# Value products by half columns and another dealing of probability copies in an attention kernel

## The chip, the cores and the metric

The kernel runs on one core of a Trainium2 chip. The metric is the device time of one execution in microseconds (us), as the median of several runs. One further execution was taken with the hardware profiler; every duration below is from it.

The core has five engines that run side by side, each in its own order, and wait for each other through semaphores: PE (TensorE, matrix products; its weight loads are listed apart as PEld), DVE (VectorE), ACT (ScalarE), POOL (GpSimd) and SP (SyncE, which issues most of the DMA transfers).

## The reference, cut to what matters

The input `x` holds 32 sequences of 32 tokens with 512 features. Three conditional layers are added to it one after another (a mixing by a picked matrix, a linear layer with a picked low-rank part, a linear layer with a picked weight). The fourth layer is attention with a paged cache, and the change lies in it:

```python
q = jnp.einsum('bsd,ed->bse', x, Wq).reshape(bsz, seqlen, HQ, D)   # HQ = 32 heads of D = 128
k = jnp.einsum('bsd,ed->bse', x, Wk).reshape(bsz, seqlen, HK, D)   # HK = 8
v = jnp.einsum('bsd,ed->bse', x, Wv).reshape(bsz, seqlen, HK, D)
# q, k: rms norm and rotary position
k_all = jnp.concatenate([kc, k], axis=1)      # 512 cached keys, then the 32 new ones
v_all = jnp.concatenate([vc, v], axis=1)
scores = jnp.einsum('bqhd,bkhd->bhqk', q, k_all) * SCALE
scores = jnp.where(valid[:, None, None, :], scores, -1e+30)
probs = jax.nn.softmax(scores, axis=-1)
o = jnp.einsum('bhqk,bkhd->bqhd', probs, v_all)
return jnp.einsum('bse,de->bsd', o, Wo)
```

All arithmetic is in float32. A float32 product appears in the trace as two matmul records.

## The kernel before, in words

**Stages.** The tokens are 1024 rows, held as 8 token tiles of 128 (`x3t`). The first part of the span computes the three conditional layers, then the projections to queries, keys and values. From 373.5 us on the attention runs. The projections are cut into chunks of 512 columns; the last chunk holds half of the values. Of that chunk only token tiles 0 and 1 are projected ahead of attention. Tiles 2 to 7 are projected inside it, as "fills": four products (one for each 128 of the 512 input features) that add up in one PSUM bank, the tile `qkv` with tag `f`. ACT copies the bank to `vs` (line 318), and SP stores `vs` to DRAM two steps later (line 323). That tag has one buffer, so the first product of the next token tile waits for ACT's copy.

**Steps.** Attention goes through 256 units, one for each batch b (32) and key head g (8), in the loop at line 1248; step n = 8b + g. All engines follow the order written in the loop. In step n:

- PE computes the scores of unit n: one product of 288 columns (line 1019) and one of 256 (line 1020) into `s_ps`, which has one buffer, so that the next scores wait until DVE has read it.
- DVE adds the mask and finds the row's least value, `low` (line 1028); ACT takes the exponential into `pr` (line 1044). Four units make a quad, so a batch has two quads, q = 0 and 1.
- On steps n < 37 PE does the fill, if there is one (`fill`, line 1231).
- For the quad that was finished before step n - n % 4, the piece j = n % 4 is turned: DVE transposes 32 x 32 blocks of all four units into `turned` (line 1057), and four copies, one for each group of 32 partitions, put them into `placed` in their right places (`place`, line 1052). The copies are dealt out to ACT (line 1069), POOL (line 1071) and DVE (line 1073). `turned` has two buffers.
- POOL gathers the probabilities of the new keys when j = 0 (`pq`, line 1080), and PE flips them when j = 2 (line 1084).
- From step 37 on PE does a share of the output projection (line 1174), most often one product of 512 columns a step.
- From step 8 on PE does the values of unit n - 8: four products of 128 columns (line 1097), with `placed` as the weights. So the values of step 8b + 8 are the first to need quad 0 of batch b, whose last piece is turned in step 8b + 7; those of step 8b + 12 need quad 1, whose last piece is turned in step 8b + 11.
- After the fourth unit of a quad PE adds the new values (line 1117, in steps 8b + 3), and DVE computes `rden` (line 1131) and scales the result into `os` (line 1133). The PSUM banks of a batch's result are one buffer, so the first values of the next batch wait for `os`. In the next step or later DVE transposes `os` to `ot` (line 1154). In the last step of a batch DVE writes the `mask` of the next (line 218).
- From batch 2 on POOL issues four index DMAs in steps 8b to 8b + 3, one for each chunk of the cached values `vt` (line 252); the first waits until the values of batch b - 2 have been used.

**The fills before.** There are 24 products of 512 columns. Steps 0 to 9 have one each, then the odd steps from 11 to 35 and step 36; the even steps from 10 to 34 are in `EMPTY` and have none.

**The copies before.** Of the four copies of a piece, ACT does the first `on_act`; the rest go to POOL (quad 0, and all of batch 0) or DVE. With one letter a copy (A ACT, P POOL, D DVE): quad 0 is A A P P, quad 1 A A D D and its last piece A A A D; in batch 0 it is A P P P and A A P P.

Of the kernel before, what the change touches and what calls it, by code (L numbers as in the profile page):

```python
# [20 lines left out]
P = 128  # L21
B, S, HID = 32, 32, 512
# [5 lines left out]
NT = B * S // P  # L28
BT = P // S
KC = HID // P  # L30
# [4 lines left out]
NCH = (HQ + 2 * HK) // REP  # L35
# [3 lines left out]
QUAD = 4  # L39
# [20 lines left out]
def cond_resid_kernel(  # L60
# [237 lines left out]
    def x3t(t: int):  # L298
        return x3_all[:, :, t * P : (t + 1) * P]
# [5 lines left out]
    ws = {}  # L305
# [2 lines left out]
        ws[c] = wqps[c % 2].tile([P, KC, HID], F32, tag="wq", name=f"wq_{c}")  # L308
        eng.dma_start(out=ws[c], in_=w_qkv[c])

    def project_part(ps, c: int, t: int, k: int):
        nc.tensor.matmul(
            ps, x3t(t)[:, k, :], ws[c][:, k, :], start=(k == 0), stop=(k == KC - 1)
        )

    def copy_values(ps, c: int, t: int):
        vs = vsp.tile([P, HID], F32, tag="vs", name=f"vs_{c}_{t}")
        nc.scalar.copy(vs, ps)
        return vs
# [5 lines left out]
    def project(c: int, t: int, slots=()):  # L325
        ps = accumulator(f"qkv_{c}_{t}", True)
        for k in range(KC):
            project_part(ps, c, t, k)
        for slot in slots:
            flush(slot)  # L330
        store_values(copy_values(ps, c, t), c, t, nc.gpsimd)
# [720 lines left out]
    def place(b: int, q: int, j: int):  # L1052
        if j == 0:
            placed[b, q] = tp.tile([P, QUAD, L // P, P], F32, tag="placed", name=f"placed_{b}_{q}")
        pr = prs[b, q][:, :, :L].rearrange("p u (c j s) -> p j u c s", j=P // S, s=S)[:, j]
        part = tp.tile([P, QUAD, L // P, S], F32, tag="turned", name=f"turned_{b}_{q}_{j}")
        nc.vector.transpose(part, pr)  # L1057

        on_pool = q == 0 or b == 0
        if b == 0:  # L1060
            on_act = 1 + q
        else:
            on_act = 3 if q == 1 and j == QUAD - 1 else 2
        for i in range(P // S):
            dst = placed[b, q][j * S : (j + 1) * S, :, :, i * S : (i + 1) * S]
            src = part[i * S : (i + 1) * S]
            dst, src = (a.rearrange("p u c s -> p (u c) s") for a in (dst, src))
            if i < on_act:
                nc.scalar.copy(dst, src)  # L1069
            elif on_pool:  # L1070
                nc.gpsimd.tensor_copy(dst, src)  # L1071
            else:
                nc.vector.tensor_copy(dst, src)  # L1073
# [129 lines left out]
    LAG = 8  # L1203
# [17 lines left out]
    units = [(b, g) for b in range(B) for g in range(HK)]  # L1221
    N = len(units)

    fills = [(t, k) for t in range(2, NT) for k in range(KC)]
    FILLED = 37
    EMPTY = tuple(n for n in range(LAG + 2, FILLED) if n % 2 == 0)
    EMPTY = EMPTY[: FILLED - len(fills)]
    filled, unstored = {}, {}
    WO_AT = [*range(7, 35, 3), *range(FILLED + 4, FILLED + 16, 2)]

    def fill(n: int):
        if n < FILLED and n not in EMPTY:
            t, k = fills.pop(0)
            if k == 0:
                filled[t] = ps_p.tile([P, HID], F32, tag="f", name=f"qkv_{NCH - 1}_{t}")
            project_part(filled[t], NCH - 1, t, k)
            if k == KC - 1:
                unstored[n + 2] = copy_values(filled.pop(t), NCH - 1, t), NCH - 1, t, nc.sync

    order = {  # L1240
# [6 lines left out]
    with tc.manual_schedule(engines=order):  # L1247
        for n in range(N + LAG):
            b, g = divmod(n, HK)
# [8 lines left out]
            if n < N:  # L1258
# [21 lines left out]
                exponentials(*scored)  # L1280
            flip_kept(n)
            fill(n)
            if n in unstored:
                store_values(*unstored.pop(n))
# [4 lines left out]
            if QUAD <= n < N + QUAD:  # L1289
                bq, i = divmod(n - QUAD, HK)  # L1290
                q, j = divmod(i, QUAD)
                if j == 0:
                    gather_new(bq, q)
                if j == 2:
                    flip_new(bq, q)
                place(bq, q, j)
# [89 lines left out]
```

## Time and profile before

| | |
|---|---|
| median of 3 runs | 1139.4 us (1138.61 to 1139.44) |
| profiled execution: time, span | 1139.8 us, 1138.0 us |
| granted TensorE clock | 1.0 |
| busy share of the span | PE 99%, PEld 64%, DVE 71%, ACT 66%, POOL 49% |
| attention begins, step 8, step 37 | 373.5 us, 390.66 us, 469.31 us |

The span is the time from the first to the last instruction that the profile shows; the execution's own time has 1.8 us around it. Matmuls overlap, and the end of one is modelled, so the distance from one start to the next tells more of PE than a duration. In a row of a timeline the brackets name how long the engine was idle before it and what ended that. In a group's row stand the count, the busy time, the mean of one in ns, and the idle time of the engine just before the group.

### The profile page before, as it was taken

Reading aid. Unit: us, or ns where it says so; the run is one execution under the profiler, and the core shown is the slowest. Engines: PE = TensorE matmul, PEld = TensorE weight load, DVE = VectorE, ACT = ScalarE, POOL = GpSimd, SP = SyncE. Lnnn points to the kernel's source line nnn. Section 1 sums busy time; section 2 is a strip of 40 time slices with the busy share of each in tenths; the row PEclk is TensorE's granted clock in tenths of the full one; section 3 lists DMA queues with packets and bytes.
Section 4 is the critical chain, followed back from the end, with each engine's and each line's share of the span. In section 5 each row is a group of like instructions: output and inputs, shape, how many; then the busy total and the mean of one; then the engine's idle time right before and its main releaser. Section 6 shows DMA issues by size and latency. Waiting matters only on the chain. (4 is left out here: it accounts for less than half of the span.)

```text
span 1138.0 us, 18994 instructions
## 1 busy us (share of the span) xinstructions
PE 1122.4 (99%) x5432; PEld 730.1 (64%) x5432; DVE 807.5 (71%) x1670; ACT 752.8 (66%) x1900; POOL 559.0 (49%) x719
## 2 busy tenths in 40 slices
PE   8999999999999999999999999999999999999998
PEld 5554444444444577777777777777777777777766
DVE  2510688886977487777778868877877777877851
ACT  1211377576666688777777777877777877777750
POOL 3411689899897544533443344334533443344310
PEclk9999999999999999999999999999999999999999
DMA  8998447688786587888667756765776676766610
GB/s 319 392 419 347 176 133 220 174 234 229 197 232 169 159 272 267 271 308 284 216 217 243 248 190 230 262 229 178 243 251 223 200 239 224 240 202 214 222 29 10
DMA packets 173354, 259.24 MB, mean 228 GB/s; under 512 B 31522, under 2 KB 130466, under 8 KB 168770
## 3 DMA queue, kind: packets, MB, share of 16 engines
q1 hardware_dynamic: 152226, 184.22, 51.0%
q0 software_dynamic: 20016, 71.97, 17.7%
q10 hardware_dynamic: 1008, 1.84, 0.4%
q8 instruction: 44, 0.72, 0.3%
q14 instruction: 60, 0.49, 0.1%
HBM read 228.46 MB, written 37.88 MB: 234 GB/s over the span
## 5 line engine op out<-in xcount | busy, mean ns | idle before, releaser
L1069 ACT COPY placed<-turned 32x512 f32<-32x512 f32 x539 | 332.8, 617 | 31.4 <-DVE turned L1057 24.0
L1097 PEld LDWEIGHTS o_ps<-vt,placed 128*128 128x128 f32 x2048 | 267.0, 191 | 118.5 <-issue 89.4
L1028 DVE CUSTOM_DVE_ANT_0 pr<-s_ps,mask,rq 128x544 f32<-128x544 f32 x256 | 200.6, 784 | 132.5 <-PE s_ps L1020 124.0
L1044 ACT ACTIVATE pr<-pr,low 128x544 f32<-128x544 f32 x256 | 192.2, 751 | 132.7 <-DVE low L1028 130.8
L1071 POOL COPY placed<-turned 32x512 f32<-32x512 f32 x268 | 163.6, 611 | 230.8 <-DVE turned L1057 164.1
L1097 PE MATMUL o_ps<-vt,placed 128*128 128x128 f32 x2048 | 270.4, 275 | 5.6 <-ACT placed L1069 2.8
L1174 PE MATMUL f_ps<-wo,ot 128*128 128x512 f32 x480 | 241.3, 594 | 0.7
L1057 DVE STREAM_TRANSPOSE turned<-pr 128x512 f32<-128x512 f32 x256 | 178.7, 698 | 0.1
L1019 PE MATMUL s_ps<-kt,qt 128*128 128x288 f32 x512 | 174.4, 422 | 1.4 <-DVE low L1028 0.5
L1020 PE MATMUL s_ps<-kt,qt 128*128 128x256 f32 x512 | 152.3, 379 | 0.4 <-issue 0.4
L252 POOL DMA_INDIRECT vt<-in_v_cache_dram,v_idx x128 | 128.0, 1000 | 36.6 <-issue 25.4
L1020 PEld LDWEIGHTS s_ps<-kt,qt 128*128 128x128 f32 x512 | 97.2, 190 | 27.5 <-DMA kt<-in_k_cache_dram 0.8
L434 POOL TENSOR_TENSOR ra<-ra,rs 128x512 f32<-128x512 f32 x80 | 103.9, 1306 | 10.6 <-DVE rs L429 6.4
L1174 PEld LDWEIGHTS f_ps<-wo,ot 128*128 128x128 f32 x480 | 85.8, 190 | 28.6 <-issue 13.9
L1073 DVE COPY placed<-turned 32x512 f32<-32x512 f32 x217 | 94.6, 436 | 5.5
L1080 POOL COPY pq<-pr 128x128 f32<-128x128 f32 x64 | 18.6, 290 | 149.4 <-PE o_ps L1097 94.6
L447 ACT ACTIVATE sq<-x 128x128 f32<-128x128 f32 x256 | 76.4, 302 | 19.3 <-DVE x L405 13.9
L1019 PEld LDWEIGHTS s_ps<-kt,qt 128*128 128x128 f32 x512 | 77.3, 191 | 17.0 <-DVE low L1028 10.6
L544 ACT COPY r<-m 128x512 f32<-128x512 f32 x80 | 46.4, 580 | 52.4 <-PE m L389 51.4
L389 PE MATMUL m<-t_pair,x_sums 128*128 128x512 f32 x160 | 75.3, 593 | 0.6 <-ACT r L544 0.6
L389 PE MATMUL m<-w_pair,x3t 128*128 128x512 f32 x160 | 75.2, 592 | 0.0
L389 PE MATMUL m<-w_pair,x_sums 128*128 128x512 f32 x160 | 72.1, 592 | 0.0
(129 smaller groups left out, 1223.6 us busy)
## 6 DMA issues: line engine op xcount, KB each, us to landing
kt<-in_k_cache_dram SPq DMA_DIRECT2D x512, 128.0 KB
wa<-in_w_adapt_dram SPq DMA_DIRECT2D x32, 1024.0 KB
q_d<-st SPq DMA_DIRECT2D x128, 128.0 KB
qt<-q_d SPq DMA_DIRECT2D x64, 256.0 KB
w_pair<-in_w_qkv_dram SPq DMA_DIRECT2D x20, 512.0 KB
o_d<-in_w_o_dram SPq DMA_DIRECT2D x16, 512.0 KB
wo<-o_d SPq DMA_DIRECT2D x16, 512.0 KB
k_d<-st SPq DMA_DIRECT2D x32, 128.0 KB
```

Source lines behind the costliest of these rows:

```text
L252: nc.gpsimd.indirect_dma_start(out=vts[b][:, c, :], out_offset=None, in_=v_cache, in_offset=bass.IndirectOffsetOnAxis(ap=v_idx[:, at : at ...
L389: nc.tensor.matmul(ps, of[:, k], by[:, k], start=(not more and k == 0), stop=(k == KH - 1), skip_group_check=more,)
L434: nc.gpsimd.tensor_tensor(u.a, u.a, u.s, ALU.add)
L1019: nc.tensor.matmul(ps[:, first:L], q, kt4[:, :N_LOW, g, :], start=True, stop=True)
L1020: nc.tensor.matmul(ps[:, L : first + LT], q, kt4[:, N_LOW:, g, :], start=True, stop=True)
L1028: nc.vector.tensor_tensor_reduce(pr, ps[:, first : first + LT], mask, rqs[b][:, g // QUAD, u : u + 1], 3.0e38, ALU.add, ALU.min, low,)
L1044: nc.scalar.activation(pr, pr, AF.Exp, bias=low, scale=-1.0, accum_out=dens[quad][:, u : u + 1])
L1057: nc.vector.transpose(part, pr)
L1069: nc.scalar.copy(dst, src)
L1071: nc.gpsimd.tensor_copy(dst, src)
L1097: nc.tensor.matmul(po, pt[:, c, :], vt[:, c, g * D : (g + 1) * D], start=(c == 0 and q == 0), stop=(c == L // P - 1 and q == 1),)
L1174: nc.tensor.matmul(pfs[t][:, :HID], ots[t, h // HALF][:, h % HALF, :], wo(h), start=(h == 0), stop=(h == (HQ if t < NT - 1 else HALF) - 1),)
```

## The change

Each product of the fills is done in two halves of 256 columns, first all four of the left half of a token tile, then all four of the right half, in the same PSUM bank. There are now 48. Every step from 0 to 36 has one, and steps 0 to 7, 8, 16 and 24 have two. ACT's copies to `vs` are now in steps 3, 7, 14, 21, 28 and 36; they were in steps 3, 7, 13, 21, 29 and 36. The first half product of the next token tile follows in the very next step.

In batches 0 to 4 the four copies of a piece are dealt out otherwise: quad 0 is A P P P with the last piece A D D P, quad 1 is A A P P. So in each of batches 1 to 4 ACT does 12 copies where it did 17, DVE 2 where it did 7, and POOL 18 where it did 8. In batch 0 only the last piece of quad 0 differs. From batch 5 on all is as before.

The orders of the engines differ in nothing else, but that SP's store of `vs` of one token tile stands one step later, behind the key loads of a batch.

```diff
-    def project_part(ps, c: int, t: int, k: int):
+    def project_part(ps, c: int, t: int, k: int, cols=slice(0, HID)):
         nc.tensor.matmul(
-            ps, x3t(t)[:, k, :], ws[c][:, k, :], start=(k == 0), stop=(k == KC - 1)
+            ps[:, cols],
+            x3t(t)[:, k, :],
+            ws[c][:, k, cols],
+            start=(k == 0),
+            stop=(k == KC - 1),
         )
...
-        on_pool = q == 0 or b == 0
-        if b == 0:
-            on_act = 1 + q
+        if b <= BT:
+            by = "AAPP" if q == 1 else "ADDP" if j == QUAD - 1 else "APPP"
+        elif q == 0:
+            by = "AAPP"
         else:
-            on_act = 3 if q == 1 and j == QUAD - 1 else 2
+            by = "AAAD" if j == QUAD - 1 else "AADD"
         for i in range(P // S):
...
-            if i < on_act:
+            if by[i] == "A":
                 nc.scalar.copy(dst, src)
-            elif on_pool:
+            elif by[i] == "P":
                 nc.gpsimd.tensor_copy(dst, src)
             else:
                 nc.vector.tensor_copy(dst, src)
...
-    fills = [(t, k) for t in range(2, NT) for k in range(KC)]
+    fills = [(t, h, k) for t in range(2, NT) for h in range(2) for k in range(KC)]
     FILLED = 37
-    EMPTY = tuple(n for n in range(LAG + 2, FILLED) if n % 2 == 0)
-    EMPTY = EMPTY[: FILLED - len(fills)]
+    DOUBLE = (*range(LAG), 8, 16, 24)
...
     def fill(n: int):
-        if n < FILLED and n not in EMPTY:
-            t, k = fills.pop(0)
-            if k == 0:
+        for _ in range((1 + (n in DOUBLE)) * (n < FILLED)):
+            t, h, k = fills.pop(0)
+            if (h, k) == (0, 0):
                 filled[t] = ps_p.tile([P, HID], F32, tag="f", name=f"qkv_{NCH - 1}_{t}")
-            project_part(filled[t], NCH - 1, t, k)
-            if k == KC - 1:
+            project_part(filled[t], NCH - 1, t, k, slice(h * HID // 2, (h + 1) * HID // 2))
+            if (h, k) == (1, KC - 1):
                 unstored[n + 2] = copy_values(filled.pop(t), NCH - 1, t), NCH - 1, t, nc.sync
```

## The prediction

> **What bounds the kernel now.** I read the page first, then the windows over the stretch that the change touches, then the timelines of TensorE, VectorE and GpSimd around one batch border, then the answer on the tile `placed`.
>
> The page: engine totals and the groups of the copies that are dealt out anew.
>
> ```profile
> PE 1122.4 (99%) x5432; PEld 730.1 (64%) x5432; DVE 807.5 (71%) x1670; ACT 752.8 (66%) x1900; POOL 559.0 (49%) x719
> ...
> L1069 ACT COPY placed<-turned 32x512 f32<-32x512 f32 x539 | 332.8, 617 | 31.4 <-DVE turned L1057 24.0
> ...
> L1071 POOL COPY placed<-turned 32x512 f32<-32x512 f32 x268 | 163.6, 611 | 230.8 <-DVE turned L1057 164.1
> ...
> L1073 DVE COPY placed<-turned 32x512 f32<-32x512 f32 x217 | 94.6, 436 | 5.5
> ```
>
> PE fills 99% of the span, so only PE's idle time or PE's work can change the time. A copy costs 617 ns on ACT, 611 on POOL, 436 on DVE. The windows (steps 8 to 15, 16 to 23, 24 to 31, 32 to 36; then a stretch that the change does not touch on PE):
>
> ```profile
> 390.66:412.18 21.52, 21.04 (x124) 15.94 (x125) 13.69 (x30) 17.23 (x36) 11.70 (x21) 1.00 0.73 225
> 412.18:434.00 21.82, 19.79 (x124) 15.47 (x123) 17.58 (x38) 18.33 (x37) 9.51 (x15) 1.00 0.79 271
> 434.00:455.27 21.27, 20.11 (x124) 15.54 (x123) 17.70 (x38) 17.91 (x37) 9.50 (x15) 1.00 0.91 306
> 455.27:469.31 14.04, 13.16 (x85) 10.14 (x84) 12.81 (x28) 11.37 (x23) 5.77 (x8) 1.00 0.89 312
> 469.31:490.00 20.69, 20.69 (x121) 15.41 (x120) 15.48 (x35) 16.23 (x35) 9.50 (x14) 1.00 0.81 271
> ```
>
> Length, then busy time of PE, PEld, DVE, ACT, POOL. The last window has no idle PE; the four before it have 4.55 us (78.65 less 74.10). Where it lies, PE's timeline shows (steps 15 and 16):
>
> ```profile
> 410.00 0.59 PE L1020 MATMUL s_ps<-kt,qt 128*128 128x256 f32 x2
> 410.44 1.02 PE L312 MATMUL qkv<-wq,x3t 128*128 128x512 f32 x2
> 411.29 1.05 PE L1097 MATMUL o_ps<-vt,placed 128*128 128x128 f32 x8
> 412.18 0.65 PE L1019 MATMUL s_ps<-kt,qt 128*128 128x288 f32 x2
> 412.67 0.59 PE L1020 MATMUL s_ps<-kt,qt 128*128 128x256 f32 x2
> 414.30 1.13 PE L1097 MATMUL o_ps<-vt,placed 128*128 128x128 f32 x8 [1.04 <-ACT placed L1069]
> ```
>
> Starts, not durations, give PE's price, since matmuls overlap: a whole fill 0.85 us (410.44 to 411.29; 0.86 elsewhere), values 0.89, scores 0.92 (with a 256-column pair at 0.43), a flip 0.11. Step 16 has no fill, and its values wait 1.04 us for the last copies of `placed`. DVE and POOL at that border:
>
> ```profile
> 411.34 0.71 DVE L1057 STREAM_TRANSPOSE turned<-pr 128x512 f32<-128x512 f32 x1
> 411.98 0.14 DVE L1131 RECIPROCAL rden<-den 128x4 f32<-128x4 f32 x1
> 412.38 0.69 DVE L1133 TENSOR_TENSOR os<-o_ps,rden 128x512 f32<-128x512 f32 x1 [0.27 <-PE o_ps L1097]
> 412.99 0.69 DVE L218 TENSOR_SCALAR mask<-key_i,len_f 128x544 f32<-128x544 int16 x1
> 413.81 0.78 DVE L1028 CUSTOM_DVE_ANT_0 pr<-s_ps,mask,rq 128x544 f32<-128x544 f32 x1
> ```
>
> ```profile
> 412.11 1.27 POOL L1071 COPY placed<-turned 32x512 f32<-32x512 f32 x2 [0.80 <-DVE rden L1131]
> 413.65 1.02 POOL L252 DMA_INDIRECT vt<-in_v_cache_dram,v_idx  x1 [0.27 <-POOL placed L1071]
> 414.72 0.29 POOL L1080 COPY pq<-pr 128x128 f32<-128x128 f32 x1
> 415.18 1.06 POOL L252 DMA_INDIRECT vt<-in_v_cache_dram,v_idx  x1 [0.17 <-issue]
> 416.55 0.94 POOL L252 DMA_INDIRECT vt<-in_v_cache_dram,v_idx  x1 [0.30 <-issue]
> ```
>
> Here lie the two things that decide: DVE is nearly solid from the transpose to the next `low`, and POOL has four index DMAs in each batch from the third on, each about 1.0 us busy with 0.3 between.
>
> **Part 1, the halves.** 24 products become 48 of half the columns. By the 256-column scores row a half takes 0.43, so 48 of them cost what 24 whole ones do (0.86): nothing is added. Each loads its weights again; eight value matmuls in 0.89 us already load weights at that pace, so the loads stay covered; without that cover it is at most 24 times two loads of 0.19, 9 us, which I exclude as the narrower 128-column row does not show it. Steps 0 to 8 keep the same work. From 9 to 36 a step costs 0.92 + 0.43 + 0.89 = 2.24, with a flip 2.35, with the new values 2.99 (0.65, and 0.10 that PE loses in starting afresh, as after each wait: 414.30 to 415.27 is 0.97 for 0.89). Before, it was 2.67 with a fill; without, 1.97 to 2.07, since the next scores wait for `low` (its start 1.12 after the scores', its result 0.84 later).
>
> The accumulator has one buffer, so the next chunk's first half waits for ACT's copy `vs`. Chunks now end at 14 and 21 with the next at 15 and 22 (before, a step lay between). ACT does the exponential first: it starts 1.94 after the scores, takes 0.84, the copy 0.57: 3.35. PE is there at 3.27 and 3.16: with latency and restart +0.25 in step 15, +0.35 in 22. Behind that fill PE's values and scores queue. A chunk's end at 28 hides behind the wait of that step (below). Of SP only one store of `vs` moves behind a batch's loads; its rows are read from batch 16 on: nothing.
>
> **Part 2, the copies.** In batches 1 to 4 each batch takes five copies from ACT (3.1 us), five from DVE (2.2) and gives POOL ten (6.1). None is on PE; what counts is when the fourth piece of a quad is ready. Two borders per batch:
>
> *Into step 8b* (letters A D D P). From the scores of 8b-1: `low` starts at 1.12, the transpose at 1.83, ends at 2.54; the two DVE copies, new here, 0.85: 3.39; reciprocal 0.14, `os` 0.69: 4.22; mask 0.50; `low` 4.72; scores of 8b+1 at 5.56. Values of 8b wait for `os` too (same PSUM banks), to 4.3, where before ACT's second copy came last. A DVE copy beside a POOL copy is in no row. Bounds: 0 and 0.61 (one POOL copy first, twice in the worst case). Nearest: the mask, 0.50 in its eight uses beside no POOL copy and 0.70 in the 24 beside one. I take 0.20: 5.76, rounded to 5.8 for the two steps, against 5.85, 5.42 and 5.55 measured at 16, 24 and 32. So this wait is not removed; it passes from ACT to DVE. What is gained is that the doubles at 16 and 24 lie under it.
>
> *Into step 8b+4* (A A P P instead of A A A D). ACT's third copy goes. POOL now alternates: index DMA 0.3 + 1.0, two copies 1.27: 2.57 a step against PE's 2.24 to 2.99. From the scores of 8b (24 or 32): `low` at 2.7, `ot` and the transpose, done at 4.8; copies of the first piece done at 6.1; then three times 2.57: 13.85. PE: 3.56 + 2.34 + 2.35 + 2.99 + 1.35 = 12.59. So the values of 28 and 36 wait 1.3 for POOL, and behind them queue PE's next scores, on which `low` and the exponential wait. At 20 `ot` falls away: 12.9 against 12.3, 0.6. Step 12 has no DMAs: 0.04 as before. Step 44 is covered by whole output products (2.67 a step). The fourth `vt` chunk is issued about 12 us after step 8b starts and lands 6.3 to 8.7 later, before the 22.5 or so at which it is read.
>
> At step 8 the last piece drops two POOL copies: it is ready at 392.7 instead of 393.4, PE comes at 392.97: 3.20 instead of 3.78.
>
> **The sum**, steps before against after:
> - 8 to 15: 21.52; 3.20 + 2.24 + 2.35 + 2.99 + 2.28 + 2.24 + 2.35 + 2.50 = 20.15: -1.37
> - 16 to 23: 21.82; 3.30 + 2.34 + 2.35 + 2.99 + 2.94 + 2.24 + 2.70 + 2.24 = 21.10: -0.72
> - 24 to 31: 21.27; 3.56 + 2.34 + 2.35 + 2.99 + 3.64 + 2.24 + 2.35 + 2.24 = 21.71: +0.44
> - 32 to 36: 14.04; 3.56 + 2.34 + 2.35 + 2.99 + 3.64 = 14.88: +0.84
>
> Together -0.8 us: span 1138.0 to 1137.2, the profiled execution 1139.8 to 1139.0. Its time lies 0.4 above the median 1139.4, so the forecast is 1138.6.
>
> [...] The mask shows 0.46 at its fastest, 0.69 at the median over its 32 uses. [...]
>
> **Rivals.**
> - *POOL keeps up.* If the 0.3 between DMAs hides beside copies and these take 0.61, its turn is 2.22: ready at 12.75, wait 0.16 instead of 1.3, none at 20: -3.1 further, 1135.5. For it: the 0.3 is issue time, not work. Against: it stood there with POOL otherwise idle.
> - *PE alone bounds.* Without any wait steps 8 to 36 need 19.22 three times and 11.96: 69.6 against 78.65, so 1130.4. Against: DVE's 5.56 at three borders alone.
> - *POOL is slower than its median* (the other side). Its place is steps 16 to 19, 24 to 27, 32 to 35. With copies at 0.70 (three took 2.11 at 391.29, beside a mask) and DMAs at 1.19 + 0.3 (longest in these batches), its turn is 2.89, the waits 1.7, 2.35 and 2.35 instead of 0.6, 1.3, 1.3: +3.2, so 1141.8. It decides from about 2.65 on (slower than before); from 2.88 by more than can be measured.
> - *It comes out even*: the gains of part 1 and the borders cancel, 1139.4.
>
> **How the numbers follow.** Three runs lie within 0.83 us; 0.2%, 2.3 us, is about what a measurement of this kernel can tell from no change. Forecast 0.48, even 0.17, POOL keeps up 0.18, PE alone 0.05, POOL slower 0.12. Faster by over 2.3 us: POOL keeps up, PE alone and the lower edge of the forecast, 0.26; slower by over 2.3: most of the slow-POOL case, 0.10; within 0.64. The range runs from POOL keeping up (1135.3) to most of the slow case (1141.3); DVE's bound of 0.61 at three borders (+1.2) lies inside.
>
> **What would show it.** Right: in steps 9 to 36 fills of 128x256 at 0.43 from start to start; steps of 2.24 inside a batch; PE idle at 16, 24 and 32 ended by DVE `os`, at 20, 28 and 36 by POOL's `placed`, about 0.6 and 1.3 long; steps 37 on unchanged. Wrong: no POOL wait at 28 and 36 (then faster), DVE copies of 0.6 and more beside POOL's, half fills costing over 0.5, or `vt` landing late at 24, 32 or 40.

## The result and the profile after

The changed kernel takes 1209.9 us (median of 5 runs, 1209.45 to 1212.13) beside 1139.4 us for the kernel before (5 runs, 1138.61 to 1139.67): ratio 1.0622, 95% interval 1.0611 to 1.0634. The forecast was 1138.6. The change costs 70 us where nearly nothing was expected. The profiled execution of the changed kernel took 1212.1 us, its span is 1210.3, and its mean granted clock 0.972.

The page of the changed kernel: the engine totals, the granted clock over the span in 40 slices of 30 us, and the groups of copies.

```profile
PE 1131.2 (93%) x5480; PEld 745.9 (62%) x5480; DVE 800.9 (66%) x1652; ACT 739.0 (61%) x1880; POOL 581.8 (48%) x757
...
PEclk9999999999999977887999999999999999999999
...
L1074 ACT COPY placed<-turned 32x512 f32<-32x512 f32 x519 | 319.8, 616 | 72.2 <-DVE turned L1061 63.7
L1076 POOL COPY placed<-turned 32x512 f32<-32x512 f32 x306 | 187.0, 611 | 297.1 <-DVE turned L1061 175.0
L1078 DVE COPY placed<-turned 32x512 f32<-32x512 f32 x199 | 88.0, 442 | 5.1
```

PE's busy time has risen by 8.8 us only, the span by 72.3. A POOL copy still costs 611 ns; POOL is busy 22.8 us more, far from 72. So no work has become dear: PE stands idle. Where, the steps tell. Starts of steps after, less before: +0.4 us at step 8, -0.8 at 16, then +19.0 at 24, +37.4 at 32, +55.1 at 40, +72.4 at 48, and it stays there to the end. The loss lies in four batches, and in each of them nearly all in one step: 20, 28, 36 and 44 take 22.27, 19.51, 19.47 and 18.78 us. The four windows of the prediction became 20.31 (forecast 20.15), 41.62 (21.10), 39.70 (21.71) and 31.04 (14.88).

PE's timeline around step 20 of the changed kernel:

```profile
423.80 0.59 PE L312 MATMUL qkv<-wq,x3t 128*128 128x256 f32 x2
443.18 2.07 PE L1102 MATMUL o_ps<-vt,placed 128*128 128x128 f32 x8 [18.79 <-POOL placed L1076]
445.04 1.17 PE L1023 MATMUL s_ps<-kt,qt 128*128 128x288 f32 x2
```

After a half fill PE idles 18.79 us for the last copy of `placed` on POOL, at the very place where the prediction put 0.6. Why is POOL so late? Its timeline over the same steps:

```profile
412.70 1.02 POOL L252 DMA_INDIRECT vt<-in_v_cache_dram,v_idx  x1 [0.27 <-POOL placed L1076]
413.77 0.49 POOL L1085 COPY pq<-pr 128x128 f32<-128x128 f32 x1
419.52 1.25 POOL L1076 COPY placed<-turned 32x512 f32<-32x512 f32 x2 [5.26 <-DMA vt<-in_v_cache_dram,v_idx]
421.05 0.97 POOL L252 DMA_INDIRECT vt<-in_v_cache_dram,v_idx  x1 [0.28 <-POOL placed L1076]
428.65 1.25 POOL L1076 COPY placed<-turned 32x512 f32<-32x512 f32 x2 [6.63 <-DMA vt<-in_v_cache_dram,v_idx]
430.17 0.95 POOL L252 DMA_INDIRECT vt<-in_v_cache_dram,v_idx  x1 [0.27 <-POOL placed L1076]
435.81 1.25 POOL L1076 COPY placed<-turned 32x512 f32<-32x512 f32 x2 [4.70 <-DMA vt<-in_v_cache_dram,v_idx]
437.34 0.96 POOL L252 DMA_INDIRECT vt<-in_v_cache_dram,v_idx  x1 [0.27 <-POOL placed L1076]
441.87 1.25 POOL L1076 COPY placed<-turned 32x512 f32<-32x512 f32 x2 [3.58 <-DMA vt<-in_v_cache_dram,v_idx]
```

Read it by the brackets. Each pair of copies waits 3.6 to 6.6 us for the transfer of `vt` that POOL issued just before, though a copy of `placed` from `turned` reads and writes nothing of `vt`. The next index DMA stands behind that pair on POOL, so issue, landing and copies form one chain: from one DMA to the next it takes 8.35, 9.12 and 7.17 us, and 5.78 from the last to the end of its copies, at 443.12. PE starts at 443.18.

The answers on waits over 411 to 600 us (in total, times, longest): the first line is of POOL, the second of PE, and the third, the landing times, of the line of the index DMA over 405 to 560.

```profile
POOL placed L1076 <- DMA vt<-in_v_cache_dram,v_idx: 72.5, 16, 6.6
PE o_ps L1102 <- POOL placed L1076: 65.7, 4, 18.8
DMA to landing us min/median/max: 3.9/5.6/7.5
```

Sixteen waits, four in each of four batches, 72.5 us; four waits of PE, 65.7. The rest comes after each wait, as the windows over step 20 show (length; busy time of PE, PEld, DVE, ACT, POOL; granted clock, DMA share, GB/s):

```profile
425.00:430.00 5.00, 0.00 (x0) 0.00 (x0) 0.07 (x1) 0.00 (x0) 1.21 (x2) 0.97 0.79 268
430.00:435.00 5.00, 0.00 (x0) 0.00 (x0) 2.71 (x6) 2.07 (x4) 0.95 (x1) 0.50 0.66 213
435.00:440.00 5.00, 0.00 (x0) 0.00 (x0) 0.71 (x1) 0.62 (x1) 2.17 (x3) 0.50 0.18 33
440.00:445.00 5.00, 1.82 (x8) 1.82 (x9) 0.00 (x0) 0.00 (x0) 2.88 (x6) 0.50 0.20 80
445.00:450.00 5.00, 5.00 (x25) 3.95 (x24) 2.18 (x6) 1.93 (x4) 1.88 (x4) 0.83 0.01 3
```

While PE idles, the granted clock falls to 0.50. The first values afterwards take 1.86 from start to start (443.18 to 445.04) instead of 0.89. The mean of 0.83 over 445 to 450 puts the rise back to 1.0, as an estimate, at about 446.7, 3.5 us after PE has started again. Steps 20 and 21, 28 and 29, 36 and 37, 44 and 45 are together 74.8 us longer than without the wait (the like steps of the forecast or of before: 4.58, 4.58, 5.01 and 6.30 us). Less the 65.7 this leaves 9.1, or 2.3 us at each wait, for the slow restart. PE stops at 424.4, and the mean of 0.97 over 425 to 430 puts the fall, as an estimate, at about 429.7, 5.3 us later. At the waits of steps 28, 36 and 44 the fall comes 4.5, 2.3 and 2.1 us after PE's last product, and the rise 5.5, 3.4 and 4.3 us after PE has started again (estimates from the mean clock in windows of 1 us); the first values take 1.86, 1.86 and 1.87.

The list of POOL's instructions in the program as it was built, with the semaphores that each waits for, shows that the wait is written into the program. `DMASW` is a semaphore that one of POOL's own transfers raises: in the trace POOL idles 5.26 us, until `vt` lands, before the copy that waits for `DMASW3`. The first index DMAs of attention in the changed kernel (the batch's number is left out of the tile names):

```
L252  DMACopy    vt_3887<-in_v_cache_dram,v_idx 128x1024    [waits PE_49,Pool_49]
L1085 TensorCopy pq_1_3901<-pr_4_3747 128x128               [waits Activation_49]
L1076 TensorCopy placed_1_3903<-turned_1_0_3904 32x16x32    [waits DMASW3_49,DVE_49,Pool_49]
L1076 TensorCopy placed_1_3903<-turned_1_0_3904 32x16x32
L252  DMACopy    vt_3887<-in_v_cache_dram,v_idx 128x1024    [waits Pool_49]
L1076 TensorCopy placed_1_3903<-turned_1_1_3923 32x16x32    [waits DMASW4_49,DVE_49]
```

In the kernel before, the four index DMAs stand with only `pq` between them (quad 1 was dealt to ACT and DVE), and one copy behind them, the first of quad 0, waits for all four landings (DMASW3 to 6). In the trace of before the last of the four lands 0.1 to 3.6 us before that copy starts, so the wait hardly shows. The copy `pq`, with 128 partitions, waits for no landing, and no copy of `placed` on ACT or DVE does.

### The profile page after: what moved, and what is told of

Same layout as the page of the kernel before. It is cut to its first block, busy times and chain, and to the rows that moved or that the text cites. A ratio compares the mean times of both kernels' runs of the same rounds, so it can differ in the third digit from the quotient of the medians.

```text
span 1210.3 us, 19116 instructions
## 1 busy us (share of the span) xinstructions
PE 1131.2 (93%) x5480; PEld 745.9 (62%) x5480; DVE 800.9 (66%) x1652; ACT 739.0 (61%) x1880; POOL 581.8 (48%) x757
## 5 line engine op out<-in xcount | busy, mean ns | idle before, releaser
L1102 PEld LDWEIGHTS o_ps<-vt,placed 128*128 128x128 f32 x2048 | 271.0, 194 | 176.2 <-issue 85.8
L1074 ACT COPY placed<-turned 32x512 f32<-32x512 f32 x519 | 319.8, 616 | 72.2 <-DVE turned L1061 63.7
L1102 PE MATMUL o_ps<-vt,placed 128*128 128x128 f32 x2048 | 274.7, 278 | 69.8 <-POOL placed L1076 65.7
L1076 POOL COPY placed<-turned 32x512 f32<-32x512 f32 x306 | 187.0, 611 | 297.1 <-DVE turned L1061 175.0
L1078 DVE COPY placed<-turned 32x512 f32<-32x512 f32 x199 | 88.0, 442 | 5.1
```

Source lines behind the costliest of these rows:

```text
L1102: nc.tensor.matmul(po, pt[:, c, :], vt[:, c, g * D : (g + 1) * D], start=(c == 0 and q == 0), stop=(c == L // P - 1 and q == 1),)
```

## The experiments

Theory (landing): in this program a POOL copy of `placed` that reads above partition 0 of `turned` and stands behind index DMAs waits for their landing; that makes the loss. Rivals: the halves; POOL's load, whatever its copies read; DVE's and POOL's copies side by side; the DMAs' traffic. In the diffs, `-` is the changed kernel. The first four below ran on a chip where the kernel before took 1142.4 us (17 runs), the next four where it took 1139.6 (11), the last three where it took 1142.1 (27); each ratio is to the runs on its own chip, and need not be the quotient of the two medians.

**Part 1 alone.** The halves, with the copies dealt as before.

```diff
-        if b <= BT:
-            by = "AAPP" if q == 1 else "ADDP" if j == QUAD - 1 else "APPP"
...
+        on_pool = q == 0 or b == 0
...
+        by = "A" * on_act + ("P" if on_pool else "D") * (4 - on_act)
```

> Only the half products and their steps; the copies dealt as before. The theory of the landings (a POOL copy of probabilities that reads partitions above 0 waits until the index DMAs issued before it on POOL have landed; 4 batches at about 18 us) expects none of the long waits, since POOL makes no copies between its index DMAs here: by the prediction's steps 1138 us, 1136 to 1140. If the half products were the cause, it stays near 1210. If it were the lower granted clock by itself, brought on by the halves, also well above 1140.

Measured: 1142.1 us, ratio 0.9998 (0.9989 to 1.0006). The halves are not the cause. Counted from step 8, this kernel is 1.1 us ahead of the kernel before at step 48 of its profile, and step 55 gives that back: it takes 5.19 instead of 3.11, by a wait for keys (`kt`) of 2.4 us.

**Part 2 alone.** Whole fills as before, the copies dealt as after.

> Only the new dealing of the copies in batches 0 to 4; the products of the last chunk whole and in the steps of before. The theory of the landings expects the whole loss: values of steps 20, 28, 36 and 44 wait 18 to 20 us for a copy on POOL, 1207 to 1215 us. If the half products were the cause: 1138 to 1142.

Measured: 1215.5 us, ratio 1.0646 (1.0631 to 1.0662). The new dealing alone gives the whole loss: steps 20, 28, 36 and 44 at 19.76, 18.13, 18.87 and 18.98.

**All four index DMAs in the batch's first step.**

```diff
-                if g < L // P and b >= 2:
-                    load_value_chunk(b, g)
+                if g == 0 and b >= 2:
+                    for c in range(L // P):
+                        load_value_chunk(b, c)
```

> The changed kernel, but POOL issues a batch's four index DMAs together at the start of step 8b, ahead of its copies, instead of one in each of four steps. POOL's work is the same. The theory of the landings: only the first copy of quad 1 waits, for the last of four landings, 0.3 + 5.2 + 8.3 = 13.8 us after the batch begins; four pieces at 1.27 make 18.9 against PE's 12.6, so 6.3 us a batch and about 1 of lower clock, four batches: 1160 to 1172 us. [...]

Measured: 1177.8 us, ratio 1.0314 (1.0299 to 1.0329). With the same copies and DMAs on POOL, half of the loss is gone: one wait for four landings has taken the place of four.

```profile
425.64 5.22 POOL L1076 COPY placed<-turned 32x512 f32<-32x512 f32 x8 [7.03 <-DMA vt<-in_v_cache_dram,v_idx]
```

All eight copies of quad 1 wait for it. In the profile, counted from step 8, 26.8 us of the loss are left by step 48, 6.7 a batch, about what was expected: `turned` has two buffers, so DVE's transposes stand behind the copies, and PE waits for `low` at the end of steps 19, 27, 35 and 43 (21.6 us in four waits). The time is above the expected range by what comes later: from step 48 on, in batches that the change does not touch, the steps 8b + 2 take 9.3 us more than before (178 takes 5.30 instead of 2.78). The kernel with both remedies, below, shows why.

**No index DMAs in batches 2 to 5.** Their cached values come by SP's plain transfers of contiguous rows, which are not the rows that the index picks.

```diff
+        if 2 <= b <= 5:
+            nc.sync.dma_start(out=vts[b][:, c, :], in_=v_cache[c * P : (c + 1) * P, :])
+            return
```

> The changed kernel, but the cached values of batches 2 to 5 are fetched by plain transfers of contiguous rows on SP's queue instead of by index DMAs on POOL's (so these batches use the wrong rows of the cache). The copies stay dealt as in the change. The theory of the landings: no copy has a landing to wait for; the four long waits go, and with them POOL's own 1.3 us a step: 1133 to 1141 us, unless SP's queue holds up the keys. If DVE's and POOL's copies side by side are the cause: still 1200 or more.

Measured: 1148.3 us, ratio 1.0049 (1.0034 to 1.0063). Steps 20, 28, 36 and 44 take 2.34, 2.42, 2.34 and 2.77, and PE waits for no POOL copy. It lies above the expected range; much of that is keys that come late behind the added SP transfers (PE waits 5.7 us for `kt` in four waits, the longest 3.0 at step 31). This excludes that ten copies a batch are too much for POOL, but it takes POOL's DMA issue away as well. The next pair keeps it.

**One POOL copy between the DMAs, from partition 0 or from partition 64.** In quad 1 of batches 1 to 4 POOL does one copy of each piece, at the same step, of the same shape. Only the group differs.

```diff
-        if b <= BT:
-            by = "AAPP" if q == 1 else "ADDP" if j == QUAD - 1 else "APPP"
+        if b == 0:
+            by = "AAPP" if q == 1 else "ADDP" if j == QUAD - 1 else "APPP"
+        elif b <= BT:
+            by = "PAAD" if q == 1 else "ADDP" if j == QUAD - 1 else "APPP"   # other kernel: "AAPD"
```

> In batches 1 to 4 each piece of quad 1 is dealt P A A D instead of A A P P: POOL takes one copy, the one that reads from partition 0, and the index DMAs stay one to a step. Landing theory (a POOL copy that reads above partition 0 stands behind the landing of the index DMA ahead of it; one that reads from partition 0 does not): no POOL wait for a landing in steps 16 to 19, 24 to 27, 32 to 35 and 40 to 43; only the first copies of quad 0, which do read above partition 0, wait for the four landings, 2 to 3 us in each of four batches; steps 20, 28, 36 and 44 at 2.3 to 6 us instead of about 19 to 22; time 1138 to 1152 us. Load theory (POOL simply has too much beside its index DMAs, whatever partitions its copies read): one copy instead of two between DMAs, so about half the stall is left, steps of about 10 us, time 1165 to 1180.

> In batches 1 to 4 each piece of quad 1 is dealt A A P D: POOL takes one copy of the same shape and at the same places as when it takes the first group alone, but this one reads from partition 64. Landing theory: each of these copies waits for the landing of the index DMA ahead of it, and only 0.6 us of the turn is gone against the changed kernel: steps 20, 28, 36 and 44 at 15 to 20 us, time 1195 to 1210 us. Load theory: the same time as with the first group, to 2 us.

Measured: 1143.8 us from partition 0, ratio 1.0041 (1.0026 to 1.0056); 1205.6 from partition 64, ratio 1.0570 (1.0555 to 1.0586). POOL behind its first index DMA, first with the copy from partition 0 and then from partition 64:

```profile
414.64 0.49 POOL L1087 COPY pq<-pr 128x128 f32<-128x128 f32 x1
416.60 0.86 POOL L1078 COPY placed<-turned 32x512 f32<-32x512 f32 x1 [1.46 <-DVE turned L1061]
417.62 0.97 POOL L252 DMA_INDIRECT vt<-in_v_cache_dram,v_idx  x1 [0.17 <-issue]
...
431.84 6.68 POOL L1078 COPY placed<-turned 32x512 f32<-32x512 f32 x10 [7.23 <-DMA vt<-in_v_cache_dram,v_idx]
```

```profile
420.79 0.60 POOL L1078 COPY placed<-turned 32x512 f32<-32x512 f32 x1 [5.43 <-DMA vt<-in_v_cache_dram,v_idx]
421.67 1.05 POOL L252 DMA_INDIRECT vt<-in_v_cache_dram,v_idx  x1 [0.28 <-POOL placed L1078]
429.45 0.60 POOL L1078 COPY placed<-turned 32x512 f32<-32x512 f32 x1 [6.73 <-DMA vt<-in_v_cache_dram,v_idx]
```

Load is excluded: as many copies of the same shape, and 61.8 us between them. The DMAs' traffic and the number of DVE's copies are the same in both kernels, so neither is the cause. From partition 0 the copy waits for DVE's transpose alone and the DMAs follow each other at 4.04, 2.07 and 2.83 us; only quad 0's first copy, which reads above partition 0, still waits for the landings (three times in four batches, 16.7 us). The first of these waits costs steps 23 to 25 their 4.37, 5.21 and 4.01, beside 2.24, 3.88 and 2.49 in the other kernel. From partition 64 all sixteen waits are back (73.3 us in total). One POOL copy fewer in each turn saves 4.5 of the 70.5 us.

**Both remedies.** The first group for POOL, and the four index DMAs in step 8b (`PAAD` with the edit of the third experiment).

> First group for POOL in quad 1 of batches 1 to 4 (P A A D), and the four index DMAs of a batch one after the other in the batch's first step. Landing theory: no wait of POOL for a landing that reaches PE; steps 20, 28, 36 and 44 at 2.3 to 3 us; time 0 to 4 us below the kernel before on the same chip. Load theory: four DMAs of 1.3 us in a row hold POOL 5 us in the first step and the copies behind them come late: 5 to 10 us above the kernel before.

Measured: 1150.1 us, ratio 1.0105 (1.0087 to 1.0124): a miss. In its profile steps 20, 28, 36 and 44 take 2.40, 2.34, 2.34 and 2.77, no wait for a landing reaches PE, and step 48 starts 1.6 us ahead of before. It loses later, in the batches that the change does not touch: the four DMAs of every batch now stand ahead of `pq`, which the flip in step 8b + 2 needs. From step 48 on the steps 8b + 2 together take 9.4 us more than before, and all other steps together 0.7 less. POOL in one such batch, and then the answer on PE's waits from 860 to 925 us, with step 178 (5.29 instead of 2.78):

```profile
662.91 1.20 POOL L252 DMA_INDIRECT vt<-in_v_cache_dram,v_idx  x1 [0.60 <-PE s_ps L1023]
...
666.98 0.93 POOL L252 DMA_INDIRECT vt<-in_v_cache_dram,v_idx  x1 [0.30 <-issue]
667.96 0.38 POOL L1087 COPY pq<-pr 128x128 f32<-128x128 f32 x1
```

```profile
PE pn_ps L1091 <- POOL pq L1087: 2.3, 1, 2.3
```

**The same, and no DVE copy at a border.** The last piece of quad 0 dealt `AAPP` in the first five batches instead of `ADDP`.

> As the kernel with the first group for POOL and the index DMAs in one step, and the last piece of quad 0 dealt A A P P in the first five batches, so that DVE makes no copy at a batch border. Landing theory: as there, and steps 16, 24 and 32 lose the two DVE copies that stood ahead of os (1.18 us): 0.5 to 1 us less at each, 1 to 3 us below the other; of a gain some may be given back later, as with the halves alone, where 1.2 us gained by step 48 did not last to the end. Load theory: POOL's two copies of the last piece come 0.6 later and nothing is gained.

Measured: 1153.1 us, ratio 1.0107 (1.0092 to 1.0121). Steps 16 and 24 fall from 3.74 and 3.88 to 2.75 and 2.90, as expected, but steps 18 and 26 give part of it back (3.01 and 2.63 instead of 2.35 and 2.46), and steps 35 and 36 wait for queries and keys (6.38 and 4.51). A miss too: 1 to 3 us below the kernel with both remedies were expected, and the two intervals overlap. The profiled run is the slowest of its four.

**The burst in batches 2 to 5 only.** After that one DMA to a step, as before.

```diff
-                if g < L // P and b >= 2:
-                    load_value_chunk(b, g)
+                for c in range(L // P):
+                    if b >= 2 and g == (0 if b <= BT + 1 else c):
+                        load_value_chunk(b, c)
```

> As the kernel with the first group for POOL and the index DMAs in one step, but in one step only in batches 2 to 5, and one to a step after that as before. Landing theory, and that the later loss came from the copy pq standing behind four index DMAs in each batch: the gain of 1.6 us at step 48 stays, the step 8b+2 of the later batches is as before (2.78 at 162 and 178 instead of 3.14 and 5.29), step 55 at 2.67; time 2 to 3.5 us below the kernel before on the same chip, ratio 0.997 to 0.999. Rival, that four index DMAs in a row or POOL's copies cost in some other way: 4 us and more above the kernel before, as measured with the burst in all batches.

> The same with the last piece of quad 0 dealt A A P P in the first five batches, so that DVE makes no copy at a border. If the waits of keys and queries at step 35 (3.3 and 1.4 us, with this dealing and the burst in all batches) come from the dealing: steps 35 and 36 at about 6.4 and 4.5 again, time 2 to 4 us above the version without this dealing. If they were chance of the DMA queues: 1 to 2 us below it.

> The mended dealing and the burst in batches 2 to 5, but the fills whole as in the kernel before (24 products of 512 columns, with empty steps). What the copies are worth by themselves: if the two parts add up, the halves gain what the version with halves has over this one. By the steps, the doubled steps lie under the border waits and the empty steps wait for low: 1 to 1.5 us above the version with halves, so ratio 0.998 to 1.000 to the kernel before.

Measured, each in 11 runs: with `ADDP` 1143.6 us, ratio 1.0017 (1.0006 to 1.0029); with `AAPP` 1143.1, ratio 1.0007 (0.9997 to 1.0017); with whole fills 1142.0, ratio 0.9997 (0.9988 to 1.0006). The burst in all batches was the cause of the later loss: steps 162 and 178 take 2.88 and 2.78, as before. But the gain that was expected is not there. In the profile of the first one step 48 starts 1.6 us earlier than before, and the start of step 255 lies 0.3 later, counted from step 7; four single steps of 3.17 instead of 2.77 (52, 116, 148 and 212) make most of it. The profile names no wait there, and such steps stand in a kernel without any burst too (84, 116, 148 and 212 with the halves alone). The runs of this kernel scatter more (1140.9 to 1148.7) than those of before (1140.8 to 1143.5), and the profiled one was among the lowest; what the higher ones do is not seen. With `AAPP` step 35 is at 3.09, with the same dealing and the same DMAs up to there: the waits for queries and keys there did not come from the dealing. That the halves add nothing to the mended dealing goes against the sum in the expectation. None of these versions beats the kernel before by what can be told from no change.

## Why the prediction was wrong

*The step that failed* is the turn of POOL, "index DMA 0.3 + 1.0, two copies 1.27: 2.57 a step". It priced an index DMA at what its issue costs POOL and took for granted that the copy behind it runs on. In this program the copy waits for the landing, and the turn measured 8.35, 9.12 and 7.17. The last copies for step 20 were forecast for 12.9 us after the scores of step 16 and came after 31.8 (411.35 to 443.12). (For the later batches the sum has 13.85; 6.1 and three times 2.57 are 13.81, which changes nothing.) Both POOL rivals varied the same term by 0.3 us, 2.22 and 2.89; neither asked what else the two copies could wait for. No other term had to change for the loss: with one POOL copy in each turn and the DMAs as they were, the kernel is 66.0 us above before if the copy reads from partition 64, and 4.2 if it reads from partition 0.

*The clue was in the trace of before.* The answer on the line of POOL's copies, the idle time before them and what ended it:

```profile
  PE s_ps L1020: 6.4, 2
  DMA vt<-in_v_cache_dram,v_idx: 4.2, 1
```

The second line is the clue: a copy that reads no `vt` had once waited for `vt`. Most of the 4.2 us is not the landing's: in most other batches POOL idles 3.4 to 3.9 us at that place, until DVE's `turned`. What counts is the name. The prediction asked when `vt` lands only for its reader, PE ("before the 22.5 or so at which it is read"), and in no run here does PE wait for `vt`; POOL was the other one that waited. In the timeline of before four DMAs stand in a row with no copy of `placed` between them, so the wait was covered, if only by 0.1 to 3.6 us.

*What else the waits brought.* The price of a wait was its length. Here PE idles long enough for the granted clock to fall to 0.50, and each wait costs 2.3 us on top.

*Step 44* was taken to be covered by whole output products (2.67 a step). On paper, against a turn of 2.57, it is; against 7 to 9 it took 18.78.

*The border, into step 8b.* The order of waits was right: DVE's `os` ends the wait at 16, 24 and 32. The size was low: 3.74, 3.88 and 3.88 instead of 3.30, 3.56 and 3.56. DVE's rows at the first of these borders:

```profile
411.53 1.18 DVE L1078 COPY placed<-turned 32x512 f32<-32x512 f32 x2
412.73 0.18 DVE L1136 RECIPROCAL rden<-den 128x4 f32<-128x4 f32 x1
413.01 0.69 DVE L1138 TENSOR_TENSOR os<-o_ps,rden 128x512 f32<-128x512 f32 x1
413.61 0.50 DVE L218 TENSOR_SCALAR mask<-key_i,len_f 128x544 f32<-128x544 int16 x1
414.24 0.78 DVE L1032 CUSTOM_DVE_ANT_0 pr<-s_ps,mask,rq 128x544 f32<-128x544 f32 x1
```

Steps 15 and 16 together took 6.13 us; the sum has 5.76. The two copies took 1.18 instead of 0.85, 0.33 more, where the prediction says "I take 0.20": that is 0.13 of the 0.37. Most of the rest is time between instructions that the sum put at nothing: 0.28 instead of 0.14 from the reciprocal's start to that of `os`, and 0.63 instead of 0.50 from the mask's to that of `low`. POOL's copy beside DVE's pair, from 411.56, took 0.87 instead of 0.61. At all five borders where the changed kernel has such a pair it takes 1.18, and POOL's copy, which begins 0.02 or 0.03 after DVE's first, 0.86 or 0.87. Of the prediction's bounds for the pair, nothing and 0.61, which its range also counts with, neither is shown: the measured 0.33 lies between them, and 0.20 was too small.

*What held.* Half fills cost nothing: steps 9 to 15 measured 2.34, 2.35, 2.99, 2.34, 2.24, 2.35 and 2.39 beside 2.24, 2.35, 2.99, 2.28, 2.24, 2.35 and 2.50 on paper, and step 8 took 3.30 for 3.20. The fill behind ACT's copy `vs` waited at step 22 about as said (2.61 for 2.70). The first window's sum was right to 0.16 us. Of the gains forecast for the halves, 1.1 us show at step 48 of the halves alone, and none in the time.

*What stays open.* The runs show where the wait acts and on which copies. They do not show why the program is built with it for a copy that reads above partition 0 and not for the others, nor whether the chip needs it; the wait alone was not taken away, since that could leave a race. `pq` covers all 128 partitions and has no such wait either; its first partition is 0. What the copies here show fits a rule by the first partition that is read (0 without the wait, 32 and 64 with it), but that is a reading, and no run tests it further.

## What to carry to other kernels

Before putting work between two transfers that an engine issues, find out what that work waits for on its engine, in the list of semaphores or in the trace's releasers: a wait for data that the instruction does not touch is a dependency of the program, and it may be covered now only because of where it stands. Price a queue with transfers in it twice, once by issue and once by landing (here 2.57 against 7 to 9 us a turn), and give the second a rival of its own. If an engine must copy between its own index DMAs, try which partitions the copy reads: from partition 0 instead of 64 was worth 62 us here.

## What the runs showed of the hardware

- In the programs run here, POOL's 32-partition copies wait for the landing of earlier index DMAs if they read from partition 32 or 64, and don't if they read from partition 0: sixteen waits, 73.3 us in total, in the kernel with the copy from 64, and 1205.6 us; with the copy from 0 the only such waits are three, 16.7 us in total, of copies from 32, and 1143.8 us. The wait is the program's; that the chip needs it is not shown.
- At the four waits of the changed kernel PE's granted clock fell to 0.50 some 5.3, 4.5, 2.3 and 2.1 us after the last product and rose again 3.5, 5.5, 3.4 and 4.3 us after PE had started (estimates from the mean clock in windows, for step 20 0.97 over 425 to 430 and 0.83 over 445 to 450); the first values after a wait took 1.86 or 1.87 us for 0.89.
- DVE copies and a POOL copy side by side both became longer, at all five borders of the changed kernel that have them: DVE's pair took 1.18 us for 0.85, POOL's copy 0.86 or 0.87 for 0.61.
